# Two exact and two one-pass blocks per batch instead of four and four, with the aggregation's halves in the first heads' tiles

## The chip, the cores and the metric

The kernel runs on one core of a Trainium2 chip. The metric is the device time of one execution in microseconds (us). The engines are TensorE (PE in the profile, its weight loads PEld), VectorE (DVE), ScalarE (ACT), GpSimd (POOL) and SyncE (SP), which here issues nearly all transfers. Each engine works through its own queue in order and waits on semaphores that other engines raise.

## The reference

There are 32 batches of 512 rows with 512 columns. Two layers follow each other, both with the same 512 x 512 adjacency matrix `adj` of zeros and ones.

```
q, k, v = x @ Wq + bq, x @ Wk + bk, x @ Wv + bv        # 8 heads of 64
w   = softmax(q k^T / 8 + where(adj == 0, -1e9, 0))    # per head
x   = layernorm(x + w v)
x   = layernorm(x + (adj @ x) @ W1 + b1)
```

## The kernel before

`fast_kernel` computes everything in float32 exactness on one core. All engines' orders are written out by hand (`manual_schedule`): each function issues its instructions where it is called, on each engine's queue in that order. What is reordered in the Python code is reordered on five queues at once, the transfers on SyncE's too.

The work on TensorE is of two kinds. The **exact** matmuls take plain float32 operands; two of them share the array, each in one half. They are the scores (`scores`, L569; each of its outputs is a bank of 128 x 512; a call makes 16 banks for two pairs of heads) and the attention (`attend`, L592, one call per pair of heads, one bank). The **one-pass** matmuls take operands of the type float32r, which carries fewer bits; so each operand is split into a high part, a rest and a combination (`split_high` on ScalarE L298, `split_rest` on VectorE L301, `split_both` on POOL L304), and a product is three passes of four matmuls (`three_passes`, L400) into two banks, `near` and `far`. They are the projections to q and k (eight calls of `project` per batch), the values (four of `project_values`), the aggregation with `adj` (`aggregate`, L513, four calls of eight matmuls with high and low halves of x) and the convolution with W1 (`convolve`, four calls).

PSUM has one rotation of eight banks (`bank`), used by all of these in the order of the program. A scores bank is emptied by VectorE, which adds the mask (L571); ScalarE takes the exponential of a pair (L573), and POOL adds the exponentials of four row blocks into `es` (L584, three additions per pair of heads). `fold_squares` turns `es` in squares of 32 on VectorE (L628) and reduces it (L631); the column sums pass through DRAM (`fetch_parts`) and are inverted by `add_up`. `turn_out` transposes an attention output on VectorE (L606) and sends it through DRAM; `fetch_rows` brings it back as rows, `scale_rows` (ScalarE, L663) multiplies by the inverse sums, `add_rows` (POOL, L667) adds it to x. `statistics` (VectorE, L459 and L460), `square_root`, `invert_root` and `normalise` (ScalarE, L474) are a layer norm. `split` makes the halves of x for the aggregation (ScalarE L487, POOL L491), `add_bias` (POOL, L526) adds b1 to x, and `convolve` adds its two banks to it (VectorE, L546 and L547). For the batch after next, `load_squares` loads x in squares, `turn_squares` transposes them on VectorE (L342) and `split_x` splits them.

The parts of x (`XT`) and those of the aggregated y (`YT`) live in the same three tiles named `factors`, one copy each. So x of a later batch can be split only when the convolution has read y's parts, part by part. The eight tiles `e` hold exponentials, and before the change also the transposed squares of a fold and the halves of the aggregation. The weights of the projections are streamed: three tiles `stream`, and a chunk is fetched when the projection three before it is done (`AHEAD`).

A round b of the main loop is `first_half(b)` and `second_half(b)`. On TensorE a steady round is, with the number of calls: attention of heads 0 to 3 (2), projections of batch b + 1 (4), scores of b for heads 4 to 7, projections (4), attention of heads 4 to 7 (2), values of b + 1 (4), aggregation of b - 1 (4), scores of b + 1 for heads 0 to 3, convolution of b - 1 (4). `merge` puts work of the other engines behind each of these calls.

Of the kernel before, what the change touches and what calls it, by code (L numbers as in the profile page):

```python
# [18 lines left out]
P = 128  # L19
# [163 lines left out]
def fast_kernel(ctx: ExitStack, tc, verdict, x, adj, Wq, bq, Wk, bk, Wv, bv, W1, b1, out):  # L183
# [89 lines left out]
    watched = consts.tile([P, 2, NB, GROUP], FP, name="watched")  # L273
    nc.gpsimd.memset(watched, 0.0)

    adjT = consts.tile([P, NB, N], FR, name="adjT")
    inexact = consts.tile([P, NB], FP, name="inexact")
    gap = consts.tile([P, NB, N], U8, name="gap")

# [13 lines left out]
        nc.vector.tensor_reduce(inexact[:, c:c + 1], cut, axis=AX.X, op=ALU.add)  # L293

    XT, QT, KT, V = {}, {}, {}, {}

    def split_high(high, a):
        nc.scalar.activation(high, a, AF.Copy, scale=EPSILON * SHRINK)  # L298
# [108 lines left out]
    def finish_projection(b, which, m, near, far):  # L407

        bias, store = {"q": (bq_c, QT), "k": (bk_c, KT)}[which]
        t = store[b, m] = work.tile([P, N], FP, name=which, bufs=DB)  # L410
        nc.scalar.activation(t, near, AF.Identity, bias=bias[:, m:m + 1], scale=1.0 + EPSILON)  # L411
        nc.vector.tensor_add(t, far, t)  # L412

# [63 lines left out]
    def split(b, d):  # L477

        cols = X[b][:, :, d * P:(d + 1) * P]
        if b == B - 2:  # L480
            high = work.tile([P, NB, P], FR, name="high", tag="q", bufs=DB)
            low = work.tile([P, NB, P], FR, name="low", tag="k", bufs=DB)
        else:
            halves = work.tile([P, 2, NB, P], FR, name="halves", tag="e", bufs=8)
            high, low = halves[:, 0, :, :], halves[:, 1, :, :]
        HIGHS[b, d], LOWS[b, d] = high, low
        nc.scalar.activation(high, cols, AF.Copy)  # L487
        if b == B - 2:
            nc.vector.tensor_sub(low, cols, plain(high))
        else:  # L490
            nc.gpsimd.tensor_sub(low, cols, plain(high))  # L491
# [9 lines left out]
    def split_y(b, d, pm, engine=nc.gpsimd):  # L501
        high, rest, both = (YT[b][f][:, d, :] for f in range(3))
        split_high(high, pm)
        split_rest(rest, high, pm)
        split_both(both, high, rest, engine)

    def aggregate(b, d):
        if d == 0:
            YT[b] = factors()
        pm = bank(N)  # L510
        parts = [part[:, m, :] for part in (LOWS.pop((b, d)), HIGHS.pop((b, d))) for m in range(NB)]
        for n, part in enumerate(parts):
            nc.tensor.matmul(pm, part, adjT[:, n % NB, :], start=(n == 0), stop=(n == 2 * NB - 1))  # L513
        split_y(b, d, pm)

    def split_rows(b, c):
# [36 lines left out]
    def convolution(b):  # L553
        return [(convolve, b, r) for r in range(NB)] if b >= 0 else []

    E, ES, OUT, AT, ROWS, SQUARES, PART, INVERSE, TURNED, PASSED = ({} for _ in range(10))
    PAIRS = GROUP // 2

    def scores(b, g):

# [25 lines left out]
    def attend(b, hp):  # L586
        po = bank(N)
        for j in range(NB):
            e = E.pop((b, hp, j))
            for s in range(2):  # L590
                h = 2 * hp + s
                nc.tensor.matmul(po[s * HD:(s + 1) * HD, :], V[b, j][:, h * HD:(h + 1) * HD], e[:, s, :],  # L592
                                 start=(j == 0), stop=(j == NB - 1))
        if b < B - 1:
            SQUARES[b, hp] = work.tile([P, 2, N], FP, name="e", bufs=8)
        OUT[b, hp] = po

    def turn_out(b, hp):
# [17 lines left out]
    def fold_squares(b, hp):  # L616

        if hp % PAIRS == 0:
            PART[b, hp // PAIRS] = work.tile([P, P // SQ, NB, GROUP], FP, name="part", bufs=1)
        part = PART[b, hp // PAIRS]  # L620
        es = ES.pop((b, hp))
        if b == B - 1:
            squares = [work.tile([P, N], FP, name="square", tag="turn", bufs=TURNS) for _ in range(2)]
            for s in range(2):
                nc.vector.transpose(squares[s], es[:, s, :])  # L625
        else:
            square = SQUARES.pop((b, hp))
            nc.vector.transpose(square.rearrange("p s n -> p (s n)"), es.rearrange("p s n -> p (s n)"))  # L628
            squares = [square[:, s, :] for s in range(2)]
        for s in range(2):  # L630
            nc.vector.tensor_reduce(part[:, :, :, 2 * (hp % PAIRS) + s].rearrange("p i c -> p c i"),  # L631
                                    squares[s].rearrange("p (c i f) -> p c i f", c=NB, f=SQ), axis=AX.X,
                                    op=ALU.add)
        if hp % PAIRS == PAIRS - 1:
            PASSED[b, hp // PAIRS] = passing.tile([P, P // SQ, NB * GROUP], FP, name="passed")
            nc.sync.dma_start(PASSED[b, hp // PAIRS], part.rearrange("p i c h -> p i (c h)"))
# [54 lines left out]
    def run(units):  # L691
        for unit in units:
            unit[0](*unit[1:])
# [47 lines left out]
    def survey(b, which=1):  # L741

        return [(statistics, b, which, c) for c in range(NB)] if b >= 0 else []

    def residuals(b, g):

        return [[(f, b, hp) for hp in range(g * PAIRS, (g + 1) * PAIRS)] for f in (scale_rows, add_rows)]
# [11 lines left out]
    def take_scores(b, g):  # L759
        run(scores(b, g))  # L760

    def first_half(b):

        attend(b, 0)
        turn_out(b, 0)
        attend(b, 1)
        turn_out(b, 1)
        fold_squares(b, 0)
        seen, old = survey(b - 2)[NB // 2:], norm(b - 1, 1)
        fresh, young = survey(b - 1, 0), norm(b - 1, 0)  # L770
        scaled, added = residuals(b, 0)
        squares = [(load_squares, b + 2, d) for d in range(DB // 2)]
        if b == 0:
            seen, old = [(look_for_low_half, c) for c in range(NB)], [(list,), (load_last_weight,)]
        if b == 1:
            seen = [(split_last_weight, d) for d in range(DB)]
        behind = [[(fetch_rows, b, 0)] + seen, [(fetch_rows, b, 1), (fold_squares, b, 1)] + old[:1], old[1:4],
                  [(fetch_parts, b, 0)] + old[4:],
                  [(take_scores, b, 1)] + ([(store, b - 2)] if b > 1 else []),
                  [(add_up, b, 0)] + fresh[:2], fresh[2:] + [(load, b)] + scaled[:1], young[:2] + scaled[1:],  # L780
                  added + young[2:] + squares]
        units = projections(b + 1)
        run(merge(units[:4] + [(list,)] + units[4:], behind))

    def second_half(b):

        splits, gathered = aggregation(b - 1)
        scaled, added = residuals(b, 1)
        turned, divided = turns(b + 2), splits_of_x(b + 2)
        squares = [(load_squares, b + 2, d) for d in range(DB // 2, DB)]  # L790
        early_seen = survey(b - 1) if b < B - 2 else []
        attend(b, 2)
        turn_out(b, 2)
        run(squares[:1])
        fold_squares(b, 2)
        attend(b, 3)
        fetch_rows(b, 2)
        turn_out(b, 3)
        fold_squares(b, 3)
        run(squares[1:])  # L800
        fetch_rows(b, 3)
        fetch_parts(b, 1)
        units = values(b + 1)
        if b == 0:
            run(units[:2] + [(take_scores, 1, 0)] + units[2:] + turned + divided + [(add_up, 0, 1)] + scaled + added)
            return
        run(merge(units, [splits[:1], splits[1:2], splits[2:3], splits[3:] + turned[:1]]) + biases(b - 1))
        run(merge(gathered, [turned[1:2], turned[2:3], turned[3:] + [(add_up, b, 1)]]))
        if b == B - 2:
            load(B - 1)  # L810
        take_scores(b + 1, 0)
        run(merge(convolution(b - 1)[:NB if b < B - 2 else NB // 2],
                  [scaled[:1], early_seen[:1], early_seen[1:2]]))
        run(divided + scaled[1:] + added)

    def last_halves(b):

        splits, gathered = aggregation(b - 1)
        attend(b, 0)
        turn_out(b, 0)  # L820
        fold_squares(b, 0)
        attend(b, 1)
        turn_out(b, 1)
        take_scores(b, 1)
        turn_back(b, 0)
        turn_back(b, 1)
        fold_squares(b, 1)
        fetch_parts(b, 0)
        run(survey(b - 1, 0) + norm(b - 1, 0) + convolution(b - 2)[NB // 2:] + splits)
        attend(b, 2)  # L830
        turn_out(b, 2)
        attend(b, 3)
        turn_out(b, 3)
        turn_back(b, 2)
        turn_back(b, 3)
        run([(add_up, b, 0)] + folds(b, 1) + [(fetch_parts, b, 1), (last_residual, b, 0), (last_residual, b, 1)])
        run(merge(gathered, [[unit] for unit in survey(b - 2)]) + norm(b - 1, 1))
        store(b - 2)
        run([(add_up, b, 1), (last_residual, b, 2), (last_residual, b, 3)])
# [31 lines left out]
    run(merge(values(0), [[unit] for unit in turns(1)]))  # L871
    run(splits_of_x(1))

    for b in range(B - 1):
        first_half(b)
        second_half(b)
    last_halves(B - 1)

    t = B - 1
# [57 lines left out]
```

## Time and profile before

| | |
|---|---|
| median of three runs | 2639.64 us (2638.69 to 2639.71) |
| profiled execution, its own time | 2636.07 us |
| span of the profile, first to last instruction | 2634.3 us |
| granted clock of TensorE, mean | 0.997 |
| busy: TensorE, VectorE, POOL, ScalarE | 2607.4, 2186.5, 1765.0, 1592.2 us |
| share of the chain that ended last: L400, L569, L592, L513 | 51%, 17%, 16%, 9% |
| one steady round (1500.48 to 1581.27) | 80.79 us |
| of it TensorE, VectorE, POOL, ScalarE busy | 80.24, 67.06, 55.17, 49.33 us |

A timeline row gives the start in us, the length, the engine, the line, the operation, what is written from what, its shape and the number of instructions merged into the row; a bracket tells the idle time of the engine before it and what ended it. The length of a row of matmuls reaches to the modelled end of the last one, so the step from one row's start to the next row's start is the better measure of a block.

### The profile page before, as it was taken

How to read it: one execution, taken by the hardware profiler on the slowest of the kernel's cores; microseconds unless marked ns; L12 is line 12 of the kernel's file. 1: busy time of each engine (PE TensorE's matmuls, PEld its weight loads, DVE VectorE, ACT ScalarE, POOL GpSimd, SP SyncE). 2: the span in 40 equal slices, each digit the busy share in tenths (PEclk: the TensorE clock that was granted, in tenths of full speed). 3: DMA queues.
4: the chain of work that ended last, by engine and by line, in shares of the span. 5: the costliest groups of instructions: out<-in, count | busy, mean ns of one | idle time of the engine just before them, and what ended most of it. 6: DMA issues, size and time to landing. Idle time of an engine off the chain costs nothing.

```text
span 2634.3 us, 35500 instructions
## 1 busy us (share of the span) xinstructions
PE 2607.4 (99%) x11326; PEld 1706.5 (65%) x11326; DVE 2186.5 (83%) x3529; ACT 1592.2 (60%) x2618; POOL 1765.0 (67%) x1087
## 2 busy tenths in 40 slices
PE   9999999999999999999999999999999999999997
PEld 6566666666666666666666666666666666666665
DVE  8878888878887888888888878888888888888878
ACT  4456655657556566566675565755656655657564
POOL 4557668666677676676666766666767668666673
PEclk9999999999999999999999999999999999999999
DMA  8666444665445664446644456544466444665411
GB/s 244 170 162 176 141 111 115 170 178 158 111 118 148 178 171 130 111 123 178 178 151 109 119 157 178 163 120 116 137 178 174 145 110 115 169 178 152 120 50 51
DMA packets 674273, 379.42 MB, mean 144 GB/s; under 512 B 586784, under 2 KB 590880, under 8 KB 674080
## 3 DMA queue, kind: packets, MB, share of 16 engines
q1 hardware_dynamic: 673792, 376.56, 52.1%
q8 instruction: 92, 1.51, 0.2%
q14 instruction: 101, 0.83, 0.1%
q10 hardware_dynamic: 288, 0.52, 0.1%
HBM read 302.52 MB, written 74.45 MB: 143 GB/s over the span
## 4 chain that ended last, share of the span: by engine, by line
PE 93%; DVE 3%; DMA 1%; issue 1%; POOL 1%; ACT 1%; SPq 0%; DVEq 0%; POOLq 0%; ACTq 0%
PE bank L400 51%; PE bank L569 17%; PE bank L592 16%; PE bank L513 9%; DMA stream<-kept_k 1%; DVE bnst L459 0%; DVE e L571 0%; POOL es L584 0%; DVE factors L301 0%; PE bank L534 0%; POOL factors L304 0%; DVE part L631 0%; SPq L240 0%; DMA xs<-in_adj_dram 0%; DVE square L625 0%
## 5 line engine op out<-in xcount | busy, mean ns | idle before, releaser
L400 PE MATMUL bank<-factors,stream 128*128 128x512 f32 x3012 | 707.5, 393 | 5.8 <-DVE factors L301 1.8
L400 PEld LDWEIGHTS bank<-factors,stream 128*128 128x128 f32 x3012 | 560.3, 188 | 175.5 <-issue 31.9
L584 POOL TENSOR_TENSOR es<-e 128x1024 f32<-128x1024 f32 x128 | 306.8, 2397 | 512.6 <-ACT e L573 512.6
L584 POOL TENSOR_TENSOR es<-es,e 128x1024 f32<-128x1024 f32 x256 | 614.2, 2399 | 20.1
L571 DVE SCALAR_TENSOR_TENSOR e<-gap,bank 128x512 f32<-128x512 uint8 x1024 | 617.3, 678 | 6.0 <-PE bank L569 5.9
L573 ACT ACTIVATE e<-e 128x1024 f32<-128x1024 f32 x512 | 509.9, 1050 | 43.8 <-DVE e L571 27.2
L304 POOL TENSOR_TENSOR factors<-factors,factors 128x512 fp32r<-128x512 f32 x253 | 359.6, 1436 | 201.6 <-DVE factors L301 201.2
L569 PE MATMUL bank<-q,k 64*128 64x512 f32 x2048 | 476.7, 600 | 0.9 <-DVE q L412 0.9
L592 PE MATMUL bank<-e,v 128*64 128x512 f32 x2048 | 453.6, 595 | 0.0
L569 PEld LDWEIGHTS bank<-q,k 64*128 64x128 f32 x2048 | 218.2, 186 | 229.9 <-issue 152.0
L400 PE MATMUL bank<-w,factors 128*128 128x512 f32 x1536 | 360.4, 393 | 1.8 <-DVE factors L301 1.5
L663 ACT ACTIVATE rows<-rows,zero,inverse 128x64 f32<-128x64 f32 x992 | 340.9, 426 | 31.2 <-POOL es L584 22.3
L298 ACT ACTIVATE factors<-bank 128x512 fp32r<-128x512 f32 x132 | 78.5, 597 | 462.8 <-PE bank L513 459.9
L400 PE MATMUL bank<-wv,factors 128*128 128x512 f32 x1536 | 357.8, 392 | 0.0
L400 PEld LDWEIGHTS bank<-w,factors 128*128 128x128 f32 x1536 | 285.3, 188 | 86.1 <-ACT e L573 22.7
L400 PEld LDWEIGHTS bank<-wv,factors 128*128 128x128 f32 x1536 | 285.8, 188 | 84.8 <-ACT xs L474 24.3
L592 PEld LDWEIGHTS bank<-e,v 128*64 128x64 f32 x2048 | 141.4, 137 | 278.4 <-issue 276.6
L513 PE MATMUL bank<-adjT,halves 128*128 128x512 f32 x960 | 229.6, 396 | 0.0
L474 ACT ACTIVATE xs<-xs,shift,rstd 128x512 f32<-128x512 f32 x248 | 184.1, 804 | 48.4 <-DVE shift L469 48.4
L513 PEld LDWEIGHTS bank<-adjT,halves 128*128 128x128 f32 x960 | 180.8, 188 | 43.6
L411 ACT ACTIVATE q<-bank,bq_c 128x512 f32<-128x512 f32 x128 | 87.0, 679 | 194.4 <-PE bank L400 194.4
L491 POOL TENSOR_TENSOR halves<-xs,halves 128x512 fp32r<-128x512 f32 x120 | 151.8, 1298 | 62.1 <-ACT halves L487 62.1
(101 smaller groups left out, 2504.8 us busy)
## 6 DMA issues: line engine op xcount, KB each, us to landing
stream<-kept_q SPq DMA_DIRECT2D x124, 768.0 KB, 6.0
stream<-kept_k SPq DMA_DIRECT2D x124, 768.0 KB, 4.9
xin<-in_x_dram SPq DMA_DIRECT2D x496, 64.0 KB, 2.8
turned<-attT SPq DMA_DIRECT2D x124, 256.0 KB, 2.3
rows<-turned SPq DMA_DIRECT2D x496, 64.0 KB, 3.7
xs<-in_x_dram SPq DMA_DIRECT2D x31, 1024.0 KB, 7.0
out_dram<-xs SPq DMA_DIRECT2D x31, 1024.0 KB, 5.4
part<-passed SPq DMA_DIRECT2D x256, 8.0 KB, 3.3
```

The costliest lines, as they stand in the source:

```text
L304: engine.tensor_sub(both, plain(high), plain(rest))
L400: nc.tensor.matmul(pm, left(f, d), right(f, d), start=(f != REST and d == 0), stop=(f != HIGH and d == DB - 1))
L411: nc.scalar.activation(t, near, AF.Identity, bias=bias[:, m:m + 1], scale=1.0 + EPSILON)
L474: nc.scalar.activation(row, row, AF.Identity, bias=SHIFT[t][:, slot:slot + 1], scale=RSTD[t][:, slot:slot + 1])
L491: nc.gpsimd.tensor_sub(low, cols, plain(high))
L513: nc.tensor.matmul(pm, part, adjT[:, n % NB, :], start=(n == 0), stop=(n == 2 * NB - 1))
L569: nc.tensor.matmul(ps[s], keys[:, j * P:(j + 1) * P], queries, start=True, stop=True)
L571: nc.vector.scalar_tensor_tensor(e[:, s, :], gap[:, j, :], NEG * root, ps[s], op0=ALU.mult, op1=ALU.add)
L573: nc.scalar.activation(e, e, AF.Exp, scale=1.0 / root)
L584: nc.gpsimd.tensor_add(ES[b, hp], ES[b, hp] if j > 1 else E[b, hp, 0], E[b, hp, j])
L592: nc.tensor.matmul(po[s * HD:(s + 1) * HD, :], V[b, j][:, h * HD:(h + 1) * HD], e[:, s, :], start=(j == 0), stop=(j == NB - 1))
L663: nc.scalar.activation(part, part, AF.Identity, bias=zero, scale=inverse[:, c, s:s + 1])
```

## The change

The two halves of a round become one function, `iteration`. On TensorE a steady round is now: attention of heads 0 to 3, scores of b for heads 4 to 7, four projections of b + 1, attention of heads 4 to 7, scores of b + 1 for heads 0 to 3, four projections, values, aggregation of b - 1, convolution of b - 1. The scores of b + 1 need only the first four projections, those of heads 0 to 3; q and k get their tiles in two groups of two (`q0`, `q1`, `k0`, `k1`).

The halves for the aggregation lie in the tiles of the first heads' q and k. There is room for two, so the third and fourth are made behind the first and second `aggregate`; the high halves are multiplied first. The folds' squares go to the tiles named `turn`, as two transposes of 512 columns instead of one of 1024. The sums of heads 0 to 3 are folded one phase earlier, in the round before. The statistics of the new batch stand behind the convolution, the biases behind the aggregation, one square root serves both norms of a round, and all loads of x in squares stand together behind the second `project_values`. The matrix `adjT` moves to another pool.

```diff
@@ finish_projection, split, aggregate
-        t = store[b, m] = work.tile([P, N], FP, name=which, bufs=DB)
+        t = store[b, m] = work.tile([P, N], FP, name=which, tag=f"{which}{m // PAIRS}", bufs=PAIRS)
...
-            halves = work.tile([P, 2, NB, P], FR, name="halves", tag="e", bufs=8)
-            high, low = halves[:, 0, :, :], halves[:, 1, :, :]
+        room = d // PAIRS if b == B - 2 else 0
+        high = work.tile([P, NB, P], FR, name="high", tag=f"q{room}", bufs=PAIRS)
+        low = work.tile([P, NB, P], FR, name="low", tag=f"k{room}", bufs=PAIRS)
...
-        parts = [part[:, m, :] for part in (LOWS.pop((b, d)), HIGHS.pop((b, d))) for m in range(NB)]
+        parts = [part[:, m, :] for part in (HIGHS.pop((b, d)), LOWS.pop((b, d))) for m in range(NB)]
...
+        if b < B - 2 and d + PAIRS < DB:
+            split(b, d + PAIRS)
         split_y(b, d, pm)
@@ fold_squares
-            square = SQUARES.pop((b, hp))
-            nc.vector.transpose(square.rearrange("p s n -> p (s n)"), es.rearrange("p s n -> p (s n)"))
-            squares = [square[:, s, :] for s in range(2)]
+        squares = [work.tile([P, N], FP, name="square", tag="turn", bufs=TURNS) for _ in range(2)]
+        for s in range(2):
+            nc.vector.transpose(squares[s], es[:, s, :])
@@ first_half and second_half go, and instead:
+    def iteration(b):
...
+        attend(b, 0)
+        turn_out(b, 0)
+        run(survey(b - 2)[NB - 1:])
+        attend(b, 1)
+        turn_out(b, 1)
+        if b > 0:
+            fetch_parts(b, 0)
+        take_scores(b, 1)
+        fetch_rows(b, 0)
+        fetch_rows(b, 1)
...
+            old, young = norm(b - 1, 1), norm(b - 1, 0)
+            spare = [(split_last_weight, d) for d in range(DB)] if b == 1 else []
+            roots = slice(0, 2 * NB if b > 1 else NB)
+            if b == 1:
+                run(survey(0, 0))
+            run(merge(units[:4], [[(add_up, b, 0)], folded[:1] + [(square_root, b - 1, roots)],
+                                  [(invert_root, b - 1, roots)] + old[2:] + spare[:2],
+                                  ([(store, b - 2)] if b > 1 else []) + young[2:] + spare[2:]]))
+        attend(b, 2)
+        run(folded[1:])
+        turn_out(b, 2)
...
+        load(b)
+        attend(b, 3)
+        turn_out(b, 3)
+        fetch_parts(b, 1)
+        run(scaled)
+        later = scores(b + 1, 0)
+        run(added + later)
+
+        run(merge(units[4:], [[(fetch_rows, b, 2), (fetch_rows, b, 3)], [(add_up, b, 1)], [(fold_squares, b + 1, 0)], []]))
+        units = values(b + 1)
+        run(merge(units, [splits[:1], splits[1:2] + [(fold_squares, b + 1, 1)] + squares, later_scaled,
+                          later_added]))
...
+        run(merge(gathered, [turned[:1], turned[1:2], turned[2:3], turned[3:] + biases(b - 1)]))
+        fresh, seen = survey(b, 0), survey(b - 1)
...
+            run(merge(convolution(b - 1)[:NB if b < B - 2 else NB // 2],
+                      [fresh[:2], fresh[2:], seen[:2], seen[2:3]]))
+        run(divided)
```

In the last round, `last_halves`, the folds of heads 0 to 3 and the early statistics are gone, since the round before has made them.

More of the change, by code (lines that the diff above doesn't have):

```diff
@@ L274, in fast_kernel @@
     nc.gpsimd.memset(watched, 0.0)
-    adjT = consts.tile([P, NB, N], FR, name="adjT")
+    adjT = work.tile([P, NB, N], FR, name="adjT", bufs=1)
     inexact = consts.tile([P, NB], FP, name="inexact")
@@ L295, in fast_kernel @@
     XT, QT, KT, V = {}, {}, {}, {}
+    PAIRS = GROUP // 2
     def split_high(high, a):
@@ L479, in split @@
         cols = X[b][:, :, d * P:(d + 1) * P]
[L480 to L483, printed above, removed]
-            halves = work.tile([P, 2, NB, P], FR, name="halves", tag="e", bufs=8)
-            high, low = halves[:, 0, :, :], halves[:, 1, :, :]
+        room = d // PAIRS if b == B - 2 else 0
+        high = work.tile([P, NB, P], FR, name="high", tag=f"q{room}", bufs=PAIRS)
+        low = work.tile([P, NB, P], FR, name="low", tag=f"k{room}", bufs=PAIRS)
         HIGHS[b, d], LOWS[b, d] = high, low
@@ L554, in convolution @@
         return [(convolve, b, r) for r in range(NB)] if b >= 0 else []
-    E, ES, OUT, AT, ROWS, SQUARES, PART, INVERSE, TURNED, PASSED = ({} for _ in range(10))
-    PAIRS = GROUP // 2
+    E, ES, OUT, AT, ROWS, PART, INVERSE, TURNED, PASSED = ({} for _ in range(9))
     def scores(b, g):
@@ L593, in attend @@
                                  start=(j == 0), stop=(j == NB - 1))
-        if b < B - 1:
-            SQUARES[b, hp] = work.tile([P, 2, N], FP, name="e", bufs=8)
         OUT[b, hp] = po
@@ L621, in fold_squares @@
         es = ES.pop((b, hp))
[L622 to L626, printed above, removed]
-            square = SQUARES.pop((b, hp))
-            nc.vector.transpose(square.rearrange("p s n -> p (s n)"), es.rearrange("p s n -> p (s n)"))
-            squares = [square[:, s, :] for s in range(2)]
+        squares = [work.tile([P, N], FP, name="square", tag="turn", bufs=TURNS) for _ in range(2)]
+        for s in range(2):
+            nc.vector.transpose(squares[s], es[:, s, :])
         for s in range(2):
@@ L760, in take_scores @@
         run(scores(b, g))
-    def first_half(b):
+    def iteration(b):
+        units = projections(b + 1)
+        scaled, added = residuals(b, 0)
+        later_scaled, later_added = residuals(b, 1)
+        turned, divided = turns(b + 2), splits_of_x(b + 2)
+        splits, gathered = aggregation(b - 1)
+        squares = [(load_squares, b + 2, d) for d in range(DB)]
+        folded = folds(b, 1)
         attend(b, 0)
         turn_out(b, 0)
+        run(survey(b - 2)[NB - 1:])
         attend(b, 1)
@@ L767, in first_half @@
         turn_out(b, 1)
[L768 to L772, printed above, removed]
-        if b == 0:
[L774 to L791, printed above, removed]
+        if b > 0:
+            fetch_parts(b, 0)
+        take_scores(b, 1)
+        fetch_rows(b, 0)
@@ new lines, in iteration @@
+        fetch_rows(b, 1)
+        if b == 0:
+            seen = [(look_for_low_half, c) for c in range(NB)]
+            run(merge(units[:4], [[(fold_squares, b, 1), (fetch_parts, b, 0)], seen[:2], seen[2:],
+                                  [(add_up, b, 0)] + folded[:1]]))
+        else:
+            old, young = norm(b - 1, 1), norm(b - 1, 0)
[6 more added lines that the diff above has]
+                                  ([(store, b - 2)] if b > 1 else []) + young[2:] + spare[2:]]))
@@ L792, in second_half @@
         attend(b, 2)
+        run(folded[1:])
         turn_out(b, 2)
-        run(squares[:1])
-        fold_squares(b, 2)
+        if b == 0:
+            load_last_weight()
+        load(b)
         attend(b, 3)
-        fetch_rows(b, 2)
         turn_out(b, 3)
-        fold_squares(b, 3)
-        run(squares[1:])
-        fetch_rows(b, 3)
         fetch_parts(b, 1)
+        run(scaled)
+        later = scores(b + 1, 0)
+        run(added + later)
+        run(merge(units[4:], [[(fetch_rows, b, 2), (fetch_rows, b, 3)], [(add_up, b, 1)], [(fold_squares, b + 1, 0)], []]))
@@ L803, in second_half @@
         units = values(b + 1)
[L804 to L808, printed above, removed]
+        run(merge(units, [splits[:1], splits[1:2] + [(fold_squares, b + 1, 1)] + squares, later_scaled,
+                          later_added]))
@@ L809, in second_half @@
         if b == B - 2:
             load(B - 1)
[L811 to L814, printed above, removed]
+        run(merge(gathered, [turned[:1], turned[1:2], turned[2:3], turned[3:] + biases(b - 1)]))
+        fresh, seen = survey(b, 0), survey(b - 1)
+        if b == B - 2:
+            seen = []
+        if b > 0:
+            run(merge(convolution(b - 1)[:NB if b < B - 2 else NB // 2],
+                      [fresh[:2], fresh[2:], seen[:2], seen[2:3]]))
@@ L820, in last_halves @@
         turn_out(b, 0)
-        fold_squares(b, 0)
         attend(b, 1)
@@ L826, in last_halves @@
         turn_back(b, 1)
-        fold_squares(b, 1)
         fetch_parts(b, 0)
-        run(survey(b - 1, 0) + norm(b - 1, 0) + convolution(b - 2)[NB // 2:] + splits)
+        run(norm(b - 1, 0) + convolution(b - 2)[NB // 2:] + splits)
         attend(b, 2)
@@ L872, in fast_kernel @@
     run(splits_of_x(1))
+    fold_squares(0, 0)
     for b in range(B - 1):
-        first_half(b)
-        second_half(b)
+        iteration(b)
     last_halves(B - 1)
```

## The prediction

> **What bounds the kernel now.** I read the page first: shares of busy time and the chain of waits.
>
> ```profile
> PE 2607.4 (99%) x11326; PEld 1706.5 (65%) x11326; DVE 2186.5 (83%) x3529; ACT 1592.2 (60%) x2618; POOL 1765.0 (67%) x1087
> ...
> PE 93%; DVE 3%; DMA 1%; issue 1%; POOL 1%; ACT 1%; SPq 0%; DVEq 0%; POOLq 0%; ACTq 0%
> ```
>
> TensorE is the bound, and the chain runs along it. So the order of matmuls can gain only what TensorE loses between them, and can lose whatever the other engines no longer deliver in time. Next the timeline of TensorE in one batch in the middle (start, length, ...):
>
> ```profile
> 1500.48 7.09 PE L592 MATMUL bank<-e,v 128*64 128x512 f32 x32
> 1507.50 8.45 PE L400 MATMUL bank<-factors,stream 128*128 128x512 f32 x36
> 1516.51 3.00 PE L400 MATMUL bank<-factors,stream 128*128 128x512 f32 x12 [0.55 <-DVE part L631]
> 1519.43 7.21 PE L569 MATMUL bank<-q,k 64*128 64x512 f32 x32
> 1526.57 11.17 PE L400 MATMUL bank<-factors,stream 128*128 128x512 f32 x48
> 1537.67 7.09 PE L592 MATMUL bank<-e,v 128*64 128x512 f32 x32
> 1544.69 11.17 PE L400 MATMUL bank<-wv,factors 128*128 128x512 f32 x48
> 1555.70 7.65 PE L513 MATMUL bank<-adjT,halves 128*128 128x512 f32 x32
> 1563.29 7.38 PE L569 MATMUL bank<-q,k 64*128 64x512 f32 x32
> ```
>
> The four exact blocks (L592 twice, L569 twice) stand apart, each between one-pass blocks. From start to start: attention (A) 7.02, scores (S) 7.14, four projections (P) or values (V) or convolutions (C) 11.1, aggregation (G) 7.6. The batch takes 80.8 us (TensorE busy 80.24 of 80.79 in its stretch), so only some 0.5 us is idle. Its other engines, and the one place where A stands directly before S already, the last batch:
>
> ```profile
> 2545.57 7.09 PE L592 MATMUL bank<-e,v 128*64 128x512 f32 x32
> 2552.59 7.28 PE L569 MATMUL bank<-q,k 64*128 64x512 f32 x32
> ```
>
> ```profile
> 1482.80 0.69 DVE L301 SCALAR_TENSOR_TENSOR factors<-factors,bank 128x512 fp32r<-128x512 f32 x1
> 1483.40 9.64 DVE L571 SCALAR_TENSOR_TENSOR e<-gap,bank 128x512 f32<-128x512 uint8 x16
> ...
> 1500.59 0.69 DVE L547 TENSOR_TENSOR xs<-bank,xs 128x512 f32<-128x512 f32 x1
> 1501.20 6.13 DVE L301 SCALAR_TENSOR_TENSOR factors<-factors,turn 128x512 fp32r<-128x512 f32 x4
> 1507.25 1.30 DVE L606 STREAM_TRANSPOSE attT<-bank 128x512 f32<-128x512 f32 x2
> ...
> 1520.60 9.65 DVE L571 SCALAR_TENSOR_TENSOR e<-gap,bank 128x512 f32<-128x512 uint8 x16 [0.29 <-PE bank L569]
> ```
>
> ```profile
> 1483.57 1.27 POOL L304 TENSOR_TENSOR factors<-factors,factors 128x512 fp32r<-128x512 f32 x1 [0.39 <-DVE factors L301]
> ...
> 1503.51 6.21 POOL L304 TENSOR_TENSOR factors<-factors,factors 128x512 fp32r<-128x512 f32 x4 [0.69 <-DVE factors L301]
> ```
>
> The reader is to see two things. A block of 16 masks on VectorE takes 9.64 us, 0.60 each, while TensorE makes its 16 banks in 7.14. And VectorE is free for the masks only because 12 us of projections lie between A (1500.48) and S (1519.43): it comes to A's transposes 6.8 us after A's start, behind the four splits of the next x.
>
> **What the joints give.** In the new order a batch is A, S, four P, A, S, four P, V, G, C. Starts of single matmuls: one-pass to one-pass 227 to 231 ns, last one-pass to first exact 318 (+0.09), first to second one-pass behind an exact block 336 (+0.11, the next one +0.01). A takes 7.02 whether P or S follows it (2545.57 to 2552.59). So a joint of A and S saves 0.21 us. There are 62 more joints (two in each of 31 rounds): 13.0 us saved.
>
> The Trainium skill, TensorEngine Tiling (Array Packing), Key Properties, says that a change of tiling mode drains TensorE. A and S are tiled differently (128*64 and 64*128), so by the rule A to S drains too; the trace has that step at 522 ns against 523 from A to a one-pass matmul. By the rule two of eight changes go, by the rows 0.21 us for each: the same 13.
>
> **The first scores block, S of heads 4 to 7.** It now starts 7.02 us after A, without projections between. What VectorE must do before its first mask, by the new order on its queue, counted from the start of C:
>
> POOL comes first, since the bias rows of the old batch (four L526, 1.29 each) now stand behind the aggregation's last difference, and the convolution's first sum (L546) reads row 0 after its bias. In the rows, 1482.13 (end of G) to 1484.84 (end of POOL's last difference) is 2.7 us; with one bias row 4.0. Then L546 at 4.1, L547 0.78 later, done at 5.5. Behind C0 and C1 stand two statistics each of the new batch, behind C2 two, behind C3 one of the old: 0.82 each (1511.58 to 1512.40). One convolution's pair of sums takes 1.39. So 5.5 + 1.6 + 1.4 + 1.6 + 1.4 + 1.6 + 1.4 + 0.8 = 15.3. The four splits of the next x (L301 from `turn`): the first now meets no work of POOL (0.60), the second neither (0.68 in the trace, 0.60 to the next), the third and fourth meet POOL's differences (1.76 each, 1.69 to the next): 4.6, to 19.9. Two transposes (0.61 and 0.65) and the last old statistic (0.82) make 22.0. C ends after 11.4 (11.1 and the 0.3 of the next part), so the first mask starts 10.6 to 10.7 us after A's start.
>
> TensorE comes to S at 7.1. Of eight banks two hold A's outputs until those transposes, so it makes three pairs, then waits. The eighth pair reuses the fourth's banks, free at 10.7 + 8 x 0.60 + 0.1 = 15.6; with its own 0.86 and 0.1 the next projection starts at 16.5 instead of 14.2. That is 2.3 us in each of 29 batches (2 to 30): 66.7 us. In general the loss is what the first mask lies beyond 8.4 us.
>
> Bounds: without the bias in the way VectorE comes at 9.2 (loss 0.8); with the splits at the 6.13 of the row, 12.2 (loss 3.8). I take 2.3, since both pieces are in the new order as written.
>
> The Trainium skill, TensorEngine Tiling (Array Packing), PSUM Bottleneck, warns that tiling speeds up TensorE but not the emptying of PSUM. Followed to its end each S would take VectorE's 9.64 instead of 7.14, in both blocks: 2.5 x 2 x 29 = 145 us. The trace of before shows 7.14 all the same, eight banks hiding the difference; the sum above charges only what the banks do not hide.
>
> **G directly before C.** Until now S (7.1 us) hid the splitting of y. The last difference comes 2.7 us after G, and C's twelfth matmul wants it at 11 x 0.231 = 2.5: 0.2 to 0.3 lost. The low halves of blocks 2 and 3, now made inside G, go before POOL's differences (1.30 each); by the rows they fit into G's 1.87 steps, with 0.3 to spare. In the last batch, where C follows G already, the waits are 0.90 and 0.16, with more on VectorE. Bounds 0.2 and 1.1; I take 0.3 in 30 batches: 9 us.
>
> **What I cost at nothing.** The second S (next batch, heads 0 to 3): VectorE ends the first masks at 20.3, has projections' sums, two folds (four instructions, 2.6 us each pair) and waits for ScalarE's square root and four normalised rows (0.76 each), and reaches the masks near 36.5 with TensorE there at 35.2. S hides 1.3; beyond that every us counts. Bounds 0 and 1. Folds: two transposes of 512 (0.65) instead of one of 1024 (1.2), 0.4 us a batch on VectorE, 67 of 80.8 busy. SyncE's queue: the rows' eight loads wait after the fifth projection for POOL to let go of their tiles, with three weight chunks and 16 loads of x behind them; the chunks are wanted 30 us later, x's last square about 0.5 us before its transpose. The chunks that three projections must hide (after the first and the fifth) take 5.1 median in the trace against 5.56; now fewer loads stand beside them. Cover gone: 0 to 0.5 a batch.
>
> **Ends.** In batch 1 the splits come straight before S without C or G to cover x's loads, and weight 1's split (eight L309/L312 of 0.69) with the early survey (four of 0.82) falls into the stretch before the second S. Against 4.7 us of waits in before's batch 1 I count 5 us more (0 to 8). The last batch keeps its waits, with two folds fewer ahead: 0.
>
> **Sum:** -13.0 + 66.7 + 9 + 5 = +67.7. The profiled execution: span 2634.3, its time 2636.07, so 2703.8; the median of the runs is 3.6 above it: 2707.
>
> **Rivals.**
> (1) Faster: VectorE reaches the first masks by 8.4 us after A, and the banks hide all. For it: in before it came to A's transposes at 6.8 even with splits of 6.13. Against: seven statistics now lie under C where two did, and the bias comes late. Then -13 and 0 to 9 for G to C: 2627 to 2636. It decides at 8.5 us: beyond that the joint's 0.42 a batch less 0.3 is spent.
> (2) The second S is late as well, by ScalarE's order (old rows normalised before the fourth projection's bias): 1 to 2 us more, 29 to 58: 2736 to 2765.
> (3) C after G waits as in the last batch, 1.1 instead of 0.3: 24 more, 2731.
>
> **How the numbers follow.** Forecast 0.56, its own range 2661 (first mask at 9.2, ends at 2) to 2751 (12.2); rival 1 0.17; rival 2 0.15; rival 3 0.12. The range takes in the forecast's bounds, rival 3, half of rival 2, and the case between forecast and rival 1: 2640 to 2755. A measurement here tells 0.2% (5.3 us) from nothing. Faster 0.14 (rival 1 but for its edge), same 0.04, slower 0.82.
>
> **What would show it.** Right: S of L569 behind A stretched from 7.14 to about 9.5, with idle put down to VectorE's transposes and masks; masks starting 10 to 11 us after A; the batch at 83 us; a short wait of C for L301 or L304; the second S at 7.1 to 7.2. Wrong: masks starting by 8.5 us, or both S of equal length. It fails if the splits or sums on VectorE are faster than these rows, or if POOL's bias is done earlier.

## The result and the profile after

The changed kernel takes 2743.55 us (median of 6 runs, 2740.07 to 2745.22) against 2639.23 for the kernel before: a ratio of 1.0393, 95% interval 1.0379 to 1.0406. The forecast was 2707 in a range of 2640 to 2755. The direction, the main cause and the range held; the size was 37 us short of a rise of 104.

The page of the changed kernel, the same two lines as before:

```profile
PE 2687.0 (98%) x11326; PEld 1742.0 (64%) x11326; DVE 2143.0 (78%) x3595; ACT 1521.8 (56%) x2531; POOL 1764.2 (64%) x1087
...
DVE 36%; PE 18%; ACT 18%; POOL 11%; SPq 7%; issue 6%; DMA 4%; DVEq 0%; ACTq 0%; POOLq 0%
```

The number of matmuls is the same, and no engine has more to do: VectorE was busy for 2186.5 us and is for 2143.0. But the chain of waits, 93% of it TensorE before, now runs through all engines. TensorE's busy share, 98%, hides this, since a matmul that stands in line for a bank counts as busy to its modelled end. The timeline of TensorE in one round tells it:

```profile
1466.97 2.04 PE L401 MATMUL bank<-w,factors 128*128 128x512 f32 x7
1469.76 1.20 PE L401 MATMUL bank<-w,factors 128*128 128x512 f32 x4 [0.74 <-DVE factors L302]
1471.12 8.72 PE L401 MATMUL bank<-w,factors 128*128 128x512 f32 x37 [0.17 <-POOL factors L305]
1479.78 7.09 PE L591 MATMUL bank<-e,v 128*64 128x512 f32 x32
1486.80 9.33 PE L568 MATMUL bank<-q,k 64*128 64x512 f32 x32
1496.05 11.21 PE L401 MATMUL bank<-factors,stream 128*128 128x512 f32 x48
1507.20 7.09 PE L591 MATMUL bank<-e,v 128*64 128x512 f32 x32
1514.21 7.96 PE L568 MATMUL bank<-q,k 64*128 64x512 f32 x32
1522.11 11.18 PE L401 MATMUL bank<-factors,stream 128*128 128x512 f32 x48
```

From start to start the convolution takes 12.8 here (1466.97 to 1479.78), the first scores block 9.25 (1486.80 to 1496.05), the second 7.9 (1514.21 to 1522.11). The table has the means over some 25 rounds in the middle of each trace.

| step on TensorE, us | before | after | difference |
|---|---|---|---|
| first scores of a round (heads 4 to 7) | 7.37 | 9.25 | +1.88 |
| second scores (next batch, heads 0 to 3) | 7.31 | 7.93 | +0.62 |
| convolution | 11.11 | 12.65 | +1.54 |
| aggregation | 7.58 | 7.26 | -0.32 |
| eight projections | 22.38 | 22.14 | -0.24 |
| values | 11.01 | 10.88 | -0.13 |
| attention, each of two blocks | 7.02 | 7.02 | 0 |

These make +3.35; rounds 2 to 29 take 84.23 on average, 80.81 before, so 28 x 3.43 = 96 us. Rounds 0, 1 and 30 and the tail behind it are 6.8, 1.0 and 2.2 us longer and 1.8 us shorter: together 104, which is the difference of the two spans (2738.6 and 2634.3).

VectorE in the same round shows why:

```profile
1468.42 0.71 DVE L343 STREAM_TRANSPOSE turn<-xin 128x512 f32<-128x512 f32 x1 [1.11 <-DMA xin<-in_x_dram]
1469.06 0.65 DVE L302 SCALAR_TENSOR_TENSOR factors<-factors,bank 128x512 fp32r<-128x512 f32 x1
1470.48 0.71 DVE L343 STREAM_TRANSPOSE turn<-xin 128x512 f32<-128x512 f32 x1 [0.77 <-DMA xin<-in_x_dram]
1472.34 0.69 DVE L546 SCALAR_TENSOR_TENSOR xs<-bank,xs 128x512 f32<-128x512 f32 x1 [1.14 <-POOL xs L526]
...
1483.55 4.62 DVE L302 SCALAR_TENSOR_TENSOR factors<-factors,turn 128x512 fp32r<-128x512 f32 x4
1488.09 0.70 DVE L603 STREAM_TRANSPOSE attT<-bank 128x512 f32<-128x512 f32 x1
...
1490.11 9.62 DVE L570 SCALAR_TENSOR_TENSOR e<-gap,bank 128x512 f32<-128x512 uint8 x16
...
1511.96 0.69 DVE L413 TENSOR_TENSOR k<-bank,k 128x512 f32<-128x512 f32 x1 [3.57 <-ACT k L412]
...
1516.16 9.62 DVE L570 SCALAR_TENSOR_TENSOR e<-gap,bank 128x512 f32<-128x512 uint8 x16
```

The reader is to see three places. The first masks start 10.3 us after the attention (1490.11 against 1479.78), behind the bias, the statistics and the splits. The second start 9.0 after theirs (1516.16 against 1507.20), behind a wait of 3.6 us for ScalarE. And the last split of y (1469.06) stands behind a transpose that waited 1.11 us for a load.

### The profile page after: what moved, and what is told of

It reads as the page before. It is cut to its first block, busy times and chain, and to the rows that moved or that the text cites. A ratio compares the mean times of both kernels' runs of the same rounds, so it can differ in the third digit from the quotient of the medians.

```text
span 2738.6 us, 35245 instructions
## 1 busy us (share of the span) xinstructions
PE 2687.0 (98%) x11326; PEld 1742.0 (64%) x11326; DVE 2143.0 (78%) x3595; ACT 1521.8 (56%) x2531; POOL 1764.2 (64%) x1087
## 4 chain that ended last, share of the span: by engine, by line
DVE 36%; PE 18%; ACT 18%; POOL 11%; SPq 7%; issue 6%; DMA 4%; DVEq 0%; ACTq 0%; POOLq 0%
PE bank L401 10%; DVE e L570 9%; POOL es L583 6%; SPq L232 6%; ACT e L572 6%; DVE factors L302 5%; DVE bnst L460 5%; PE bank L568 5%; ACT xs L475 4%; ACT rows L655 4%; PE bank L591 3%; DMA xin<-in_x_dram 3%; DVE xs L547 3%; DVE square L621 3%; DVE xs L546 3%
## 5 line engine op out<-in xcount | busy, mean ns | idle before, releaser
L572 ACT ACTIVATE e<-e 128x1024 f32<-128x1024 f32 x512 | 519.2, 1053 | 376.1 <-DVE e L570 343.5
L568 PE MATMUL bank<-q,k 64*128 64x512 f32 x2048 | 556.2, 622 | 8.3 <-DVE attT L603 8.1
L568 PEld LDWEIGHTS bank<-q,k 64*128 64x128 f32 x2048 | 256.3, 188 | 307.0 <-DVE e L570 116.6
L401 PE MATMUL bank<-w,factors 128*128 128x512 f32 x1536 | 385.3, 400 | 27.5 <-DVE factors L302 21.1
L299 ACT ACTIVATE factors<-turn 128x512 fp32r<-128x512 f32 x124 | 68.4, 620 | 316.6 <-PE bank L401 302.0
L413 DVE TENSOR_TENSOR q<-bank,q 128x512 f32<-128x512 f32 x128 | 86.3, 674 | 170.0 <-ACT q L412 97.3
L621 DVE STREAM_TRANSPOSE square<-es 128x512 f32<-128x512 f32 x256 | 165.8, 686 | 35.4 <-POOL es L583 35.4
L343 DVE STREAM_TRANSPOSE turn<-xin 128x512 f32<-128x512 f32 x124 | 88.2, 711 | 104.4 <-DMA xin<-in_x_dram 103.8
L413 DVE TENSOR_TENSOR k<-bank,k 128x512 f32<-128x512 f32 x128 | 85.9, 671 | 104.5 <-ACT k L412 103.5
```

Of the source, the lines that this page charges most:

```text
L401: nc.tensor.matmul(pm, left(f, d), right(f, d), start=(f != REST and d == 0), stop=(f != HIGH and d == DB - 1))
L568: nc.tensor.matmul(ps[s], keys[:, j * P:(j + 1) * P], queries, start=True, stop=True)
L572: nc.scalar.activation(e, e, AF.Exp, scale=1.0 / root)
```

## The experiments

All are compared with the kernel before on the same chip. They stand on three chips, where the kernel before took 2637.26, 2638.92 and 2639.93 us; so a difference between two kernels from different chips is good to about 3 us. In the diffs, lines are those of the changed kernel unless it is said otherwise.

### Four and two statistics moved

```diff
-            if b == 1:
-                run(survey(0, 0))
+            run(survey(b - 1, 0)[0 if b > 1 else 0:])
...
         fresh, seen = survey(b, 0), survey(b - 1)
+        if b < B - 2:
+            fresh = fresh[:0]
```

This is the edit for four; for two, the slices are `[2 if b > 1 else 0:]` and `fresh[:2]`.

> The changed kernel, but the four statistics of the new batch stand behind the first scores block instead of behind the first two convolutions. Theory (the masks start late): a scores block loses what its first mask lies beyond 8.3 us after the start of the attention before it. Four statistics take 3.3 us of VectorE, so the first masks start at 7.1 instead of 10.4 and the first scores block takes 7.2 instead of 9.25. The second gets part of it back, since the statistics now stand ahead of it: TensorE comes 2.1 earlier, VectorE only 1.7 (they fill a wait of 1.7 for ScalarE), so its masks start 9.4 after the attention instead of 9.0, and it takes 8.3 instead of 7.9. Sum -1.7 in 29 batches: 2694. Rival (scores directly behind attention are slow by themselves, paced by the masks): the first block stays at 9.2, 2743 or more.

> As the run before, with only two of the four statistics moved. Theory (masks): the first masks start 1.6 us earlier, at 8.8, and the first scores block takes 7.6. The two statistics behind it fit into the wait for ScalarE, so the second block's masks stay at 9.0 and it stays at 7.9. Sum -1.65 in 29 batches: 2695. A loss that follows the mask's start one for one would show as 9.25, 7.6 and 7.2 for none, two and four statistics moved. Rival (paced by the masks anyway): no change.

Measured: 2697.96 us with four moved (ratio 1.0222, 1.0205 to 1.0239), 2703.38 with two (1.0261, 1.0243 to 1.0278). TensorE with four moved:

```profile
1383.13 7.09 PE L591 MATMUL bank<-e,v 128*64 128x512 f32 x32
1390.15 7.37 PE L568 MATMUL bank<-q,k 64*128 64x512 f32 x32
1397.44 11.18 PE L401 MATMUL bank<-factors,stream 128*128 128x512 f32 x48
```

The first scores block takes 7.29 (1390.15 to 1397.44) directly behind the attention. So the block isn't slow for where it stands; the rival falls. The medians over the rounds make a rule with the second block among them:

| first mask after the attention's start | scores block |
|---|---|
| 8.18 (second block, old rows later) | 7.14 |
| 8.38 (four statistics moved) | 7.29 |
| 8.77 (two moved) | 7.69 |
| 9.01 (second block, changed kernel) | 7.94 |
| 10.38 (changed kernel) | 9.30 |

From 8.2 us on, each us of delay of the masks costs TensorE one us. At 8.38 VectorE no longer runs late behind its own work: with four moved it waits for the convolution's banks (1.06 us ahead of the third convolution's first sum at 1461.45), and goes from there to the masks without a pause. At 8.18 it waits for the first scores themselves, as a later run shows. Two details were wrong. With four moved the second block stayed at 7.9 (8.3 was expected): the statistics fit wholly into VectorE's waits. And the convolution, 12.65 in the changed kernel, rose to 13.65 and 13.09; why is told with the moves together.

### The transposes of x behind all splits of y

```diff
-        run(merge(gathered, [turned[:1], turned[1:2], turned[2:3], turned[3:] + biases(b - 1)]))
+        run(gathered + turned + biases(b - 1))
```

> The changed kernel, but the four transposes of x's squares stand on VectorE behind all four splits of y instead of one behind each. Theory (loads of x): the convolution's 1.5 us over 11.1 come from a split of y that stands behind a transpose whose load has not landed. Without that the convolution takes 11.4, the rest being the last split's own way: -1.25 in 30 batches, 2706; the first masks stay at 10.4, since the transposes go into the wait for the bias. Rival (POOL is late: it makes two low halves and the differences there): the convolution stays at 12.6, 2743. Second rival: the transposes now delay the convolution's sums and the first masks, so that the first scores block gets what the convolution gains: 2743.

Measured: 2719.98 us (1.0313, 1.0296 to 1.0330). The convolution, whole in one row now:

```profile
1541.14 11.62 PE L401 MATMUL bank<-w,factors 128*128 128x512 f32 x48
1552.69 7.09 PE L591 MATMUL bank<-e,v 128*64 128x512 f32 x32
```

It takes 11.55 in every round, where it took 11.75 to 15.45. In sum over the trace, the transposes waited 103.8 us for loads of x in the changed kernel and 22.0 here. POOL's work is the same, so it isn't what held the convolution. The gain is 24 us and not 37, since the second rival is there in part: the first masks start at 10.54 (median) and the first scores block takes 9.72 on average.

### The loads of x earlier

```diff
-TURNS = 6
+TURNS = 7
...
-        run(merge(units[4:], [[(fetch_rows, b, 2), (fetch_rows, b, 3)], [(add_up, b, 1)], [(fold_squares, b + 1, 0)], []]))
+        run(merge(units[4:], [[(fetch_rows, b, 2), (fetch_rows, b, 3)], [(add_up, b, 1)], [(fold_squares, b + 1, 0)], squares]))
...
-        run(merge(units, [splits[:1], splits[1:2] + [(fold_squares, b + 1, 1)] + squares, later_scaled,
+        run(merge(units, [splits[:1], splits[1:2] + [(fold_squares, b + 1, 1)], later_scaled,
```

> The changed kernel with seven tiles named turn instead of six, and the 16 loads of x's squares behind the eighth projection instead of behind the second value and its fold. They are issued some 4 us earlier, and each square is there before its transpose. Theory (loads of x): the convolution takes 11.4 instead of 12.65, -1.25 in 30 batches, 2706, the same as with the transposes moved. Rival (POOL): 12.6, 2743.

Measured: 2746.96 us (1.0404, 1.0387 to 1.0422), no gain; the convolution took 13.19. But the run didn't do what it was made for: the transposes still waited 107.1 us for the loads. SyncE's queue (start, length of the row, DMA issues):

```profile
1452.12 5.32 SPq L611 DMA_DIRECT2D rows<-turned  x8
1457.54 0.57 SPq L396 DMA_DIRECT2D stream<-kept_q  x1
1458.21 0.38 SPq L396 DMA_DIRECT2D stream<-kept_k  x1
1458.67 0.38 SPq L396 DMA_DIRECT2D stream<-kept_q  x1
1459.11 13.64 SPq L232 DMA_DIRECT2D xin<-in_x_dram  x16
```

The rows' loads wait for POOL to release their tiles (1452.12). Behind them go three weight chunks of 768 KB within 1.2 us, and behind these the loads of x, which the queue takes in only slowly: 13.64 us for 16, against 9.13 in the changed kernel. The first, issued 5 us before the aggregation's start (1464.07), landed at 1467.76, 8.65 us later. The third chunk landed at 1467.58, so the first load came 0.18 us behind it. In the changed kernel the chunks go out well ahead and the loads only behind the sums of the fold (`passed<-part`):

```profile
1454.34 0.38 SPq L396 DMA_DIRECT2D stream<-kept_q  x1
1458.84 0.32 SPq L628 DMA_DIRECT2D passed<-part  x1
1459.21 9.13 SPq L232 DMA_DIRECT2D xin<-in_x_dram  x16
```

There the third chunk landed at 1463.00 and the first load at 1463.44. So for the first loads the transfers ahead set when they land, not the place of their issue. From the sixth on they land 2.2 to 2.6 us after their own issue, and then it is the pace of the issues, 0.5 to 0.6 us each, that counts: the third transpose (1468.42) waited for the twelfth load, issued at 1465.74 and landed at 1468.34.

### The bias left out

```diff
-        run(merge(gathered, [turned[:1], turned[1:2], turned[2:3], turned[3:] + biases(b - 1)]))
+        run(merge(gathered, [turned[:1], turned[1:2], turned[2:3], turned[3:]]))
```

> The changed kernel without the bias of the second layer in batches 0 to 29 (four additions on POOL in each are left out, so those batches' output lacks b1). Theory: the convolution's first sum waits 1.1 us for the bias of its row, and VectorE is behind from there to the first masks. They start at 9.3 instead of 10.4, the first scores block takes 8.2 instead of 9.25: -1.1 in 29 batches, 2711. Rival (VectorE has slack under the convolution): no change, 2743.

Measured: 2719.41 us (1.0308, 1.0290 to 1.0325). The first masks start at 9.0 and the first scores block takes 7.9, 1.3 less than in the changed kernel. So the bias behind the aggregation does hold VectorE. The convolution gave part of it back, 13.37 for 12.65, as in the other kernels that still have the transposes between the splits.

### The old rows normalised later

```diff
-                                  [(invert_root, b - 1, roots)] + old[2:] + spare[:2],
-                                  ([(store, b - 2)] if b > 1 else []) + young[2:] + spare[2:]]))
+                                  [(invert_root, b - 1, roots)] + spare[:2],
+                                  old[2:] + ([(store, b - 2)] if b > 1 else []) + young[2:] + spare[2:]]))
```

> The changed kernel, but ScalarE normalises the four rows of the old batch behind the fourth projection's bias instead of ahead of it. Theory (ScalarE's order): in the changed kernel VectorE waits 3.6 us for that bias, comes late to the fold and the two transposes, and starts the second masks 9.0 us after the attention. Now they start by 7.9, the second scores block takes 7.15 instead of 7.9: -0.76 in 29 batches, 2721. Rival (the masks' own pace, or POOL's sums ahead of the fold): the block stays at 7.9, 2743.

Measured: 2733.47 us (1.0360, 1.0343 to 1.0378). VectorE:

```profile
1421.59 0.68 DVE L413 TENSOR_TENSOR k<-bank,k 128x512 f32<-128x512 f32 x1
...
1424.56 0.70 DVE L603 STREAM_TRANSPOSE attT<-bank 128x512 f32<-128x512 f32 x1
1427.56 0.72 DVE L603 STREAM_TRANSPOSE attT<-bank 128x512 f32<-128x512 f32 x1 [2.30 <-PE bank L591]
1428.60 9.66 DVE L570 SCALAR_TENSOR_TENSOR e<-gap,bank 128x512 f32<-128x512 uint8 x16 [0.33 <-PE bank L568]
```

The wait for ScalarE is gone, and VectorE now waits for TensorE: 2.30 us for the attention, 0.33 for the first scores. The second block takes 7.14 in every round. Of the 0.8 us a round less than half is seen in the time; the convolution rose to 13.45.

### The moves together

"Two" has the statistics (all four) and the transposes moved, "three" the old rows as well; "four" is three with the loads earlier in place of the transposes moved.

> The changed kernel with three moves together: the four statistics behind the first scores block, the transposes of x behind all splits of y, the old rows normalised behind the fourth projection. If the three losses are apart and nothing new is late, both scores blocks take 7.15 to 7.3, the convolution 11.4, and the round 80.4 to 80.7: 2632 to 2645, level with the kernel before or a little faster. If the second masks are held by something else once the first are early, 0.5 us a round more: 2655.

> As the run with three moves, but the loads of x are earlier (seven tiles) and the transposes stay one behind each split. Same expectation, 2632 to 2645; if the transposes under the convolution delay the masks in the other kernel, this one is the faster of the two.

> The changed kernel with the statistics and the transposes moved, but the old rows normalised ahead of the fourth projection as in the changed kernel. Theory (the three losses are apart when the loads no longer stand between the splits): the second scores block takes 7.9 instead of 7.14 and all else is as with three moves: +0.8 in 29 batches, 2652. That move alone brought 10 us, because the convolution gave back the rest. Rival (the moves need each other, the second masks come later still): 2665 or more.

| kernel | us | ratio and interval | convolution |
|---|---|---|---|
| two | 2650.59 | 1.0042 (1.0026 to 1.0057) | 11.55 |
| three | 2629.53 | 0.9964 (0.9951 to 0.9976) | 11.55 |
| four | 2681.39 | 1.0154 (1.0137 to 1.0171) | 13.49 |

TensorE in a round of three:

```profile
1407.45 11.62 PE L401 MATMUL bank<-w,factors 128*128 128x512 f32 x48
1419.00 7.09 PE L591 MATMUL bank<-e,v 128*64 128x512 f32 x32
1426.02 7.37 PE L568 MATMUL bank<-q,k 64*128 64x512 f32 x32
1433.32 11.17 PE L401 MATMUL bank<-factors,stream 128*128 128x512 f32 x48
1444.42 7.09 PE L591 MATMUL bank<-e,v 128*64 128x512 f32 x32
1451.44 7.21 PE L568 MATMUL bank<-q,k 64*128 64x512 f32 x32
```

Both scores blocks take their full speed, 7.30 and 7.14, and a round 80.31 instead of 84.23. From two to three, the late old rows alone, is 21 us, which is 0.8 in every round; alone they brought 10. The three moves alone sum to 46 + 24 + 10, some 79 us, together they make 114. So the losses weren't apart in the changed kernel. Part of the gap is in the scores: with the transposes alone moved, the first scores block grew by 0.47. The rest is mostly in the convolution. In all seven kernels with a transpose between two splits it takes 12.6 to 13.7 on average; in the five that have the transposes behind, 11.55 to 11.67.

Most of the rise from 12.65 to as much as 13.65 is the granted clock of TensorE. A convolution with four statistics moved, on TensorE:

```profile
1367.87 2.05 PE L401 MATMUL bank<-w,factors 128*128 128x512 f32 x7
1371.81 11.39 PE L401 MATMUL bank<-w,factors 128*128 128x512 f32 x41 [1.89 <-DVE factors L302]
1383.13 7.09 PE L591 MATMUL bank<-e,v 128*64 128x512 f32 x32
```

then this convolution, a stretch inside it, and the next convolution (start and end, length, busy time of the engines with their instructions, granted clock, DMA share, GB/s):

```profile
1367.87:1383.13 15.26, 13.36 (x50) 9.62 (x48) 9.24 (x16) 2.25 (x5) 8.03 (x7) 0.89 0.19 30
1372.75:1376.05 3.30, 3.30 (x9) 2.30 (x8) 1.46 (x3) 0.00 (x0) 3.30 (x4) 0.50 0.03 5
1452.68:1464.90 12.22, 11.85 (x50) 8.60 (x48) 8.30 (x15) 2.25 (x5) 7.56 (x6) 1.00 0.17 27
```

After a wait of 1.89 us the clock stood at half for some 3.4 us. In rounds 1 to 29 the traces have this in 1 of the changed kernel's 29 convolutions, in 9 with four statistics moved, 3 with two, 6 without the bias, 4 with the old rows later, 5 with the loads earlier and 8 in four. These 36 are all the convolutions of 14.7 us or more; the others average 12.5 to 12.9 in every one of the seven kernels. In those rounds it comes inside no convolution of the five kernels with the transposes behind, nor of the kernel before. In each of the 36 TensorE had waited 1.2 us or more at one place, but waits of up to 1.9 us also passed without it; what decides stays open. The time follows: the four runs with four statistics moved took 2691.22, 2695.72, 2700.21 and 2705.18 us at a mean granted clock of 0.995, 0.993, 0.992 and 0.989. Where the transposes are moved, the waits and the half clock are both gone. So a wait for a load was often paid twice, and a single move that leaves these waits in place looks worth less than it is.

### Where adjT lies

This kernel is the one before with one line of the change.

```diff
-    adjT = consts.tile([P, NB, N], FR, name="adjT")
+    adjT = work.tile([P, NB, N], FR, name="adjT", bufs=1)
```

> The kernel before with one line of the change alone: adjT lies in the pool work instead of among the small constants. In every kernel with that line the aggregation's matmuls follow each other at 226.8 ns, in the kernel before at 235.3. Theory (where adjT lies sets it): 227 here too, the aggregation 0.25 us shorter in 30 batches, -7 us, 2632. Rival (what sets it is the order of the halves, high first, or the tiles they lie in): 235 and no change, 2639.

Measured: 2631.00 us, ratio 0.9971 (0.9960 to 0.9983). All matmuls that read adjT, first in this kernel (minimum, median and maximum of their length in ns):

```profile
L513 PE MATMUL bank<-adjT,halves x960: 388/389/389, 181.9 to 2526.2; 128*128 128x512 f32 x192
```

then in the kernel before:

```profile
L513 PE MATMUL bank<-adjT,halves x960: 392/397/400, 181.6 to 2532.3; 128*128 128x512 f32 x192
```

They follow each other at 228.4 ns on average instead of 235.3, and the aggregation takes 7.34 instead of 7.58. So the line is worth 8 us in the old order, and three's steady round, 80.31, is to be compared with 80.60 here. Which property of the place does it stays open: the tiles laid out behind adjT move with it.

### Round 0, and the last difference of y

Both start from three. The first issues the loads of x's squares behind the eighth projection in round 0 alone (with `TURNS = 7`); the second adds:

```diff
-        split_y(b, d, pm)
+        split_y(b, d, pm, nc.vector if d == DB - 1 else nc.gpsimd)
```

> The three moves, and in round 0 alone the loads of x's squares behind the eighth projection (seven tiles named turn). With three moves the first scores block of batch 1 still takes 15.0 us instead of 7.3, its masks behind transposes that wait for those loads. They land some 5 us earlier: 2625. If they again stay behind the weight chunks in the queue: 2629.

> As the run before, and the last difference of y (the one the convolution waits for) on VectorE instead of POOL. With three moves the convolution takes 11.55 instead of 11.1: 0.17 at the fourth matmul, which waits for ScalarE's high part, and 0.14 and 0.11 at the twelfth and thirteenth, which wait for this difference. The second part goes: -0.25 in 30 batches, 7 us less than the run before. If VectorE's difference meets POOL's at the shared work on two SBUF operands, as the splits of x do (1.7 instead of 0.6), nothing is gained.

Measured: 2627.16 us (0.9952, 0.9939 to 0.9966) and 2632.47 (0.9973, 0.9962 to 0.9983). The first is no clear gain over three: the scores block of batch 1 still takes 15.2 us, and its trace has the loads again behind the weight chunks, the first landing 9.5 us after its issue. The second is a loss of 5 us. VectorE in it:

```profile
1410.97 0.69 DVE L302 SCALAR_TENSOR_TENSOR factors<-factors,bank 128x512 fp32r<-128x512 f32 x1 [1.12 <-ACT factors L299]
1411.69 1.45 DVE L305 TENSOR_TENSOR factors<-factors,factors 128x512 fp32r<-128x512 f32 x1
```

The difference takes 1.45 us there (0.69 at its shortest, POOL's 1.30), and the convolution 11.67 instead of 11.56.

## Why the prediction was right, and where it was short

**The joints.** As worked out, attention takes 7.02 with scores behind it, and the one-pass blocks lost their extra entries (values 11.01 to 10.88). The 13 us of saving can't be read off the whole by itself, since the aggregation also changed; by the table the projections and values gained 0.37 a round, 11 us.

**The first scores block** was the forecast's main term, 2.3 us in 29 batches. VectorE was put at 10.6 to 10.7 us and came at 10.38; the block took 9.25 against 7.14 in its cleanest form, 2.1, and 1.88 more than in the kernel before, 54 us of the 67 forecast. The pieces held: the bias row waited for by the first sum (1.14 us), the seven statistics, the splits at 4.6 (4.62). The moved statistics and the bias left out show them to be the cause. Two errors cancelled here: counted from C's start VectorE came at 23.1 (1466.97 to 1490.11) and not at 22.0, but C ended at 12.8 and not at 11.4, both behind the same late split. Where the transposes are moved and C takes 11.55, the masks start at 10.5, so the working stands without that luck. The point from which it costs is 8.2 us and not 8.4.

**G directly before C** is the term that was mis-sized: 0.3, measured 1.54, so 46 us instead of 9. The working took the rows of POOL's last difference and a queue of VectorE without stalls. The wait that it priced, C's twelfth matmul for POOL, is there with 0.17; the wait of C's eighth matmul for VectorE's last split, 0.74, is not in it. What failed is the step, under what I cost at nothing, "x's last square about 0.5 us before its transpose": the loads go out behind the fold's sums, the first of them land 4.2 us after their issue, behind three weight chunks, the later ones follow at the pace of the issues, 9.13 us for 16; the transposes wait, up to 1.54 us in the round shown before the first of them (1464.59), and the next split of y stands behind them in VectorE's order. I had named the chunks and judged them by when they themselves are wanted. Without that the term is 0.45 (11.55 against 11.1), near what was said.

**The second scores block** was cost at nothing, with bounds of 0 and 1. It lost 0.8. The step named the four normalised rows ahead of the fourth projection and put VectorE 1.3 us behind TensorE, just within what the banks hide. VectorE came where it was put (36.4 after A's start for 36.5, 1479.78 to 1516.16); TensorE came at 34.4 (1514.21), not at 35.2, and the working's own figures, 16.5 + 11.1 + 7.0, make 34.6. The slip hid the loss. The move of the old rows shows that they are all of it. Rival 2, which priced this at 1 to 2 us, was nearer than the forecast; that the total lies in its band, 2736 to 2765, is luck, since this block added 18 us to the forecast and the convolution 37. Rival 3 had the convolution nearly right in size and form (0.90 and 0.16 in the old last batch, 0.74 and 0.17 here), without the load as its cause.

**The ends** were put at 5 us and took 6, rounds 0 and 1 and the tail; round 30 belongs to the terms above.

**Not seen at all** was adjT's line, -8 us in the old order. It partly covered the rest, so without it the forecast would have been further off.

Rival 1, no loss at all, did not come in the changed kernel; but three's two scores blocks are what it described, and then the change in order is worth little. Three is 10 us faster than the kernel before and adjT's line alone 8, so the new order with all three repairs adds some 2 us, which these intervals don't tell from nothing: 0.29 us in each of 28 steady rounds, most of it lost again at the ends.

## What to carry to other kernels

Before two blocks of a bound engine are joined, work out for the queue that empties their banks when its first instruction can start, with everything that the new order puts ahead of it. Here 0.42 us a round was to be gained, and each us of lateness beyond the banks' slack was lost in full.

An instruction that waits for a load doesn't belong between two that the bound engine waits for, even if the load looks early. Judge its landing by what stands ahead in the same queue and by the pace of the issues, and move the waiting instruction rather than the load.

When a change has several parts, run the smallest line alone: here one declaration gave most of what the repaired version gains.

## What the hardware showed unexpectedly

The same matmuls with the same operands ran at 235.3 or 228.4 ns apart by where the tiles lie. Sixteen loads issued some 4.5 us earlier in the round landed no earlier, the first 8.65 us after its issue instead of 4.22, right behind three transfers of 768 KB. Waits of TensorE between 1.2 and 2.4 us were followed in 36 convolutions by some 3.4 us at a granted clock of 0.5; these took 14.7 to 16.6 us. And a difference of two SBUF operands on VectorE took 0.69 to 1.77 us, median 1.45, in the place tried.
